# Normalized tokens of four chunks of six, turned by VectorE squares and memory in place of TensorE

## The chip, the cores and the metric

One Trainium2 chip, one of its cores. The metric is device time in microseconds (us) for one execution of the whole kernel; lower is better.

## The reference

The input is x of shape (8, 128, 48, 48): 8 batches, 128 channels, N = 2304 positions. Everything is float32. What is computed, cut to what matters:

```python
# layer 0: causal attention over positions, with a group norm ahead of it
x0 = concat([gn(x), position embeddings])             # 160 channels
q, k, v = (leaky_relu(W @ x0 + b) for W, b in ...)    # 128 channels each
x = x + softmax(causal(q.T @ k / sqrt(128))) @ v
# layer 1: full attention of the normalized tokens with themselves, no weights
t = x as (8, 2304, 128)
n = layernorm(t)                                      # over the 128 channels of a token
t = t + softmax(n @ n.T) @ n
# then a recurrent feed-forward layer with batch norm
t = t + scan(sigmoid(wx_t + y @ V.T)), wx = batchnorm(layernorm(t) @ W.T)
```

The change concerns `n`. Full attention needs it in two arrangements: with tokens on partitions (for the product of the probabilities with n) and with channels on partitions (for the scores n @ n.T).

## The kernel before, in words

A core's memory has 128 partitions. A batch's 2304 positions are cut into NQ = 6 chunks of QC = 384 columns, a chunk into QB = 3 blocks of P = 128. For each batch the kernel runs causal attention (class `Causal`) and then full attention (class `Full`); after all batches a recurrence (from line 1499) runs in 96 segments.

**Order of work.** The order is written out by the program itself (`manual_schedule`, line 788). `stream` (lines 1466 to 1476) lists all items, and each item is one 128 x 384 block of scores: `begin` issues the score product on TensorE and the exponential on ScalarE, and LAG = 3 items later `product` issues the product with the values. Causal chunk j has 3(j+1) items, so the chunks grow from 3 to 18 items. All other work is put in chains of steps: `st.add` takes a list of (function, cost on TensorE, [(engine, us), ...]); class `Stream` (line 548) keeps an estimated clock, `st.now`, and estimated free times of the engines, and `st.tick`, called after each item, issues up to two steps whose time has come. `st.finish(chain)` issues all that is left of a chain at once, `st.advance(chain, n)` as many steps as are needed for n to be done. A step's estimate only decides where its instructions stand in the queues of the engines; what an instruction really waits for is its semaphores. Each engine, and SyncE (SP), which issues most DMAs, works through its queue in order.

**Causal attention.** `Causal.begin` (1022): scores of keys on partitions by queries in columns (L1032), exp on ScalarE into a tile p (L1034, six buffers), for the blocks on the diagonal a multiplication by triu on GpSimd (L1037). `Causal.product` (1041): the output o gathers v times p (L1043), and VectorE adds p to a running sum acc (L1054, L1058). The projections of the following chunks (`project`, 869) run beside it as chains. When a chunk is done, `after` (1061) makes a chain that takes the chunk to normalized tokens. For chunks 0 to 4 (`far`) the output is turned to tokens on partitions by VectorE, which turns each 32 x 32 square in its place (`turn_result`, L972), and by a store and four loads that move the squares (`token_major`, L980 and L986: o_d_c and to_c). Then:

- `turn` (1081) and `sums` (1087): the softmax denominators, with a small product on TensorE (dn, L1091);
- `residual` (1099): y, the tile t1t that was loaded with x at L1079, gets the attention's output divided by its denominator (L1105), and its mean and variance per token (L934 to L937);
- `rooted` (1111): the inverse root on GpSimd (L943);
- `normed` (1114): the normalized tokens, c["y"], into the tokens-on-partitions copy x_hat[b][0], tile xhT (L948);
- `back` (1122): the same with channels on partitions, into x_hat[b][1], tile xh: three 128 x 128 transposes on TensorE into the tile tb in PSUM (L953), and a copy on ScalarE (L1124);
- `shifted` (1126): GpSimd adds 1 to xhT and takes 1 from t1t (L1128, L1129).

**Full attention.** `Full.begin` (1244) issues the scores from xh alone, as weights and as columns (L1269), and `Full.product` the product with xhT (L1291). As the scores are symmetric, blocks under the diagonal are not computed again: VectorE turns squares (L1236), stores (e, L1187) and loads (g, L1179) bring the mirrored blocks, which L1279 uses; those inside a chunk go through GpSimd's queue (m, gm, L1217, L1221). While j is 0, `begin` calls `st.finish(normed_chunks[b, chunk])` ahead of each block (1247), so all steps of a causal chunk's chain are issued by the time that full attention first uses that chunk. Its own chains (`after`, 1299) make the token's second layer norm and the product with W.

`chunk_tile` (692) hands out working tiles and sees that the chain of the tile's former holder has been issued far enough.

Of the kernel before, what the change touches and what calls it, by code (L numbers as in the profile page):

```python
# [14 lines left out]
F32 = mybir.dt.float32  # L15
# [589 lines left out]
def fast_path(ctx: ExitStack, tc: tile.TileContext, x, pe, w_ffn, out, x_tok, w_qkv, w_pos, v_t, gamma_beta, flag):  # L605
    nc = tc.nc
    B, C, H, W = x.shape
    N = H * W
    P = 128
# [3 lines left out]
    QC = 384  # L613
    NQ = N // QC
    QB = QC // P
# [6 lines left out]
    dpool = ctx.enter_context(tc.tile_pool(name="dram", bufs=1, space=DRAM))  # L622
# [17 lines left out]
    SQ = 32  # L640
    R = P // SQ
# [25 lines left out]
    with ExitStack() as actx:  # L667
# [19 lines left out]
        def psum_t(name):  # L687
            return ps_t.tile([P, CH], F32, tag="t", name=name)
# [3 lines left out]
        def chunk_tile(tag, name, holder=None, steps=0, bufs=2):  # L692

            if holder is not None:
                before = holders.setdefault(tag, deque([({}, 0)] * bufs))
                old, n = before.popleft()
                before.append((holder, steps))
                if "chain" in old:
                    st.advance(old["chain"], n)
            return (work if bufs == 2 else work1).tile([P, QC], F32, tag=tag, name=name)  # L700
# [228 lines left out]
        def moments(y, name, tag):  # L929

            mv = small.tile([P, QB, 2], F32, tag=f"mv_{tag}", name=f"mv_{name}")
            for g in range(QB):
                s6 = small.tile([P, 6], F32, tag=f"st_{tag}", name=f"st_{name}_{g}")
                nc.vector.bn_stats(s6, y[:, ts(g, P)])  # L934
                nc.vector.bn_aggr(mv[:, g, :], s6)
            ve = small.tile([P, QB], F32, tag=f"ve_{tag}", name=f"ve_{name}")
            nc.vector.tensor_scalar_add(ve, mv[:, :, 1], 1e-5)  # L937
            return mv, ve
# [11 lines left out]
        def transposed(src, name):  # L950
            tp = psum_t(name)
            for g in range(QB):
                nc.tensor.transpose(tp[:, ts(g, P)], src[:, ts(g, P)], ident)  # L953
            return tp
# [9 lines left out]
        def turn_result(o, name, holder, blocks_first):  # L964

            ot = chunk_tile("o", f"ot_{name}", holder, 1)
            dst, src = ot.rearrange("p (a g c) -> p a g c", a=R, g=QB), o[:, :QC]
            if blocks_first:
                dst, src = dst.rearrange("p a g c -> p g a c"), src.rearrange("p (g a r) -> p g a r", a=R, g=QB)
            else:  # L970
                src = src.rearrange("p (a g r) -> p a g r", a=R, g=QB)
            nc.vector.transpose(dst, src)  # L972
            return ot

        def token_major(holder, ot, name, tag, steps):

            d = dpool.tile([P, QC], F32, tag=f"o_{tag}", name=f"o_d_{name}")

            def store():
                nc.sync.dma_start(d, ot)  # L980

            def load():
                holder["o"] = to = chunk_tile(tag, f"to_{name}", holder, steps, bufs=1)
                src = d.rearrange("(k r) (a f) -> a r k f", r=SQ, a=R)
                for r in range(R):
                    nc.sync.dma_start(to[ts(r, SQ)].rearrange("r (k f) -> r k f", k=R), src[r])  # L986

            return [(store, 0.0, [("", 5.0)]), (load, 0.0, [("", 5.0)])]

        def block_of(to, g):  # L990

            return to.rearrange("p (k g c) -> p g k c", g=QB, c=SQ)[:, g]

        def by_block(tile_ap):

            return tile_ap.rearrange("p (g a r) -> p a g r", a=R, g=QB)
# [4 lines left out]
        t1_tok, x_hat, normed_chunks = {}, {}, {}  # L1001

        class Causal:
# [57 lines left out]
            def after(self, j, o):  # L1061
                b = self.b
                cols = ts(j, QC)
                acc = self.sums.pop(j)[1]
                c = self.whose.pop(j)

                far = CAUSAL_FAR and j < NQ - 1
                if far:
                    ot = turn_result(o, f"c_{b}_{j}", c, False)
                    at = st.then(st.now, [("DVE", 0.57)])  # L1070
                    through = token_major(c, ot, f"c_{b}_{j}", "toc", 5)
                else:
                    o_sb = chunk_tile("o", f"oc_{b}_{j}", c, 3)
                    nc.scalar.copy(by_block(o_sb), o[:, :QC].rearrange("p (a g r) -> p a g r", a=R, g=QB))
                    at = st.then(st.now, [("ACT", 0.5)])
                    through = []

                y = t1p.tile([P, QC], F32, tag="t1t", name=f"t1t_{b}_{j}")
                nc.sync.dma_start(y, x_tok[b, j])  # L1079

                def turn():
                    ta = chunk_tile("ta", f"ta_{b}_{j}", bufs=1)
                    nc.vector.transpose(ta, acc)
                    c["parts"] = small.tile([P, R * QB], F32, tag="parts", name=f"parts_{b}_{j}")
                    nc.vector.tensor_reduce(c["parts"], ta.rearrange("p (k c) -> p k c", c=SQ), AX.X, ALU.add)

                def sums():

                    tp = psum_t(f"dn_{b}_{j}")
                    k = R * QB  # L1090
                    nc.tensor.matmul(tp[:, :k], same.rearrange("p a c -> p (a c)"), c["parts"], start=True, stop=True)  # L1091
                    own = small.tile([P, R, QB], F32, tag="ownc", name=f"ownc_{b}_{j}")
                    nc.vector.tensor_mul(own.rearrange("p a g -> p (a g)"), tp[:, :k], mine.rearrange("p a g -> p (a g)"))
                    ri = small.tile([P, QB], F32, tag="ric", name=f"ric_{b}_{j}")
                    nc.vector.tensor_reduce(ri, own.rearrange("p a g -> p g a"), AX.X, ALU.add)
                    nc.vector.reciprocal(ri, ri)
                    c["ri"] = ri

                def residual():
                    to = None if far else transposed(o_sb, f"oc_t_{b}_{j}")  # L1100
                    for g in range(QB):
                        yg = y[:, ts(g, P)]
                        if far:
                            yg = yg.rearrange("p (k c) -> p k c", k=R)
                        nc.vector.scalar_tensor_tensor(  # L1105
                            yg, block_of(c["o"], g) if far else to[:, ts(g, P)], c["ri"][:, g : g + 1], yg, ALU.mult, ALU.add
                        )
                    t1_tok[b, j] = y
                    c["mv"], c["ve"] = moments(y, f"c{b}_{j}", "l1")

                def rooted():
                    c["rs"] = root(c["ve"], f"c{b}_{j}", "l1")

                def normed():
                    if j == 0:
                        x_hat[b] = (
                            big.tile([P, NB, P], F32, tag="xhT", name=f"xhT_{b}"), big.tile([P, N], F32, tag="xh", name=f"xh_{b}")
                        )
                    c["y"] = x_hat[b][0][:, QB * j : QB * (j + 1), :].rearrange("p g c -> p (g c)")
                    normalize(c["y"], t1_tok[b, j], c["mv"], c["rs"])  # L1120

                def back():
                    tp = transposed(c["y"], f"tb_{b}_{j}")
                    nc.scalar.copy(x_hat[b][1][:, cols], tp[:, :QC])  # L1124

                def shifted():

                    nc.gpsimd.tensor_scalar_add(c["y"], c["y"], 1.0)  # L1128
                    nc.gpsimd.tensor_scalar_add(t1_tok[b, j], t1_tok[b, j], -1.0)  # L1129

                c["chain"] = normed_chunks[b, j] = st.add([
                    *through[:1],
                    (turn, 0.0, [("DVE", 1.05)]),
                    *through[1:],
                    (sums, 0.15, [("DVE", 0.55)]),
                    (residual, 0.0 if far else 0.35, [("DVE", 2.6)]),
                    (rooted, 0.0, [("POOL", 0.9)]),
                    (normed, 0.0, [("DVE", 1.1)]),
                    (back, 0.35, [("ACT", 0.5)]),
                    (shifted, 0.0, [("POOL", 1.2)]),  # L1140
                ], max(at, st.free["DVE"]) + 0.2 - st.now)

        class Full:
# [334 lines left out]
        for n in range(len(stream) + LAG):  # L1478
            if n < len(stream):
                part, j, what, first, last = stream[n]  # L1480
# [5 lines left out]
            if n >= LAG:  # L1486
                part, j, what, first, last = stream[n - LAG]
# [16 lines left out]
    with ExitStack() as rctx:  # L1504
# [32 lines left out]
        a = rc.tile([P, 1], F32, tag="bn_a", name="bn_a")  # L1537
        rsqrt(rc, a, mv[:, 1:2], 1e-5, "bn")
        nc.vector.tensor_mul(a, a, gb[:, 0:1])
        c = rc.tile([P, 1], F32, tag="bn_c", name="bn_c")  # L1540
# [17 lines left out]
        prev, warm, y = [], [], [None] * G  # L1558
# [129 lines left out]
```

## Time and profile before

| | |
|---|---|
| Time, median of 3 runs | 1742.51 us (1737.38 to 1744.68) |
| Profiled execution: time | 1747.17 us |
| Profiled execution: span from first to last instruction | 1745.5 us |
| Granted TensorE clock | 0.995 |
| Instructions | 22,358 |
| DMA packets | 214,697, of which 93,889 under 512 B |
| HBM read, written | 157.31 MB, 119.61 MB |
| TensorE transposes tb (L953) | 144, in 48 groups of three |
| ScalarE copies of tb (L1124) | 48 of 479 ns each |

The profile names the engines PE (TensorE), PEld (its weight loads), DVE (VectorE), ACT (ScalarE), POOL (GpSimd) and SP (SyncE). A row of a group of instructions has line, engine, operation, "written tile <- read tiles", shape and count, then busy us and mean ns of one, then the idle time of the engine just before them and what ended it. PE lists one product of float32 as two matmul records; a transpose of 128 x 128 is one. A letter q behind an engine's name stands for its instruction queue, so SPq is where SyncE issues DMAs. A wait for several semaphores is put down to the one that came last.

### The profile page before, as it was taken

How to read it: one execution, taken by the hardware profiler on the slowest of the kernel's cores; microseconds unless marked ns; L12 is line 12 of the kernel's file. 1: busy time of each engine (PE TensorE's matmuls, PEld its weight loads, DVE VectorE, ACT ScalarE, POOL GpSimd, SP SyncE). 2: the span in 40 equal slices, each digit the busy share in tenths (PEclk: the TensorE clock that was granted, in tenths of full speed). 3: DMA queues.
4: the chain of work that ended last, by engine and by line, in shares of the span. 5: the costliest groups of instructions: out<-in, count | busy, mean ns of one | idle time of the engine just before them, and what ended most of it. 6: DMA issues, size and time to landing. Idle time of an engine off the chain costs nothing.

```text
span 1745.5 us, 22358 instructions
## 1 busy us (share of the span) xinstructions
PE 1705.2 (98%) x6338; PEld 1094.7 (63%) x6339; DVE 1190.0 (68%) x3259; ACT 699.5 (40%) x1332; POOL 453.9 (26%) x637
## 2 busy tenths in 40 slices
PE   9999999999999999999999999999999999999986
PEld 6666666666666666666666666666666666666565
DVE  5865578656876478755786568864787656864457
ACT  3344334443344423443344433444244432444345
POOL 1232123311233112321224112332123212241206
PEclk9999999999999999999999999999999999999998
DMA  3317763378424874178632784338831686127858
GB/s 120 114 31 213 227 191 100 106 204 235 145 71 138 226 232 112 49 204 230 199 100 81 200 242 144 100 111 230 242 114 55 183 239 198 52 84 205 229 208 219
DMA packets 214697, 278.54 MB, mean 160 GB/s; under 512 B 93889, under 2 KB 178786, under 8 KB 214052
## 3 DMA queue, kind: packets, MB, share of 16 engines
q1 hardware_dynamic: 204396, 255.11, 50.0%
q0 software_dynamic: 9936, 21.51, 4.4%
q8 instruction: 52, 0.85, 0.2%
q14 instruction: 81, 0.66, 0.1%
q10 hardware_dynamic: 232, 0.40, 0.1%
HBM read 157.31 MB, written 119.61 MB: 159 GB/s over the span
## 4 chain that ended last, share of the span: by engine, by line
PE 89%; DMA 5%; DVE 2%; POOL 1%; SPq 1%; issue 1%; ACT 0%; POOLq 0%; DVEq 0%; ACTq 0%
PE s L1032 17%; PE o L1043 17%; PE s L1269 16%; PE o L1291 16%; PE o L1279 10%; DMA g<-e 3%; PE pj L895 3%; PE z L1601 2%; PE o L1287 2%; PE wx L1369 2%; DMA t2x<-t_d 1%; PE pj L898 1%; POOL gm L1221 1%; PE tb L953 1%; PE of_t L953 1%; SPq L1187 1%
## 5 line engine op out<-in xcount | busy, mean ns | idle before, releaser
L1271 ACT ACTIVATE p<-s,shift 128x384 f32<-128x384 f32 (+2 forms) x504 | 274.8, 551 | 544.5 <-PE s L1269 480.1
L1034 ACT ACTIVATE p<-s 128x384 f32<-128x384 f32 (+2 forms) x504 | 230.2, 460 | 395.3 <-PE s L1032 331.2
L1043 PE MATMUL o<-p,vT 128*128 128x384 f32 (+2 forms) x1008 | 377.8, 456 | 4.6 <-POOL p L1037 4.6
L1032 PE MATMUL s<-q,k 128*128 128x384 f32 (+2 forms) x1008 | 381.4, 460 | 0.1
L1269 PE MATMUL s<-xh 128*128 128x384 f32 (+2 forms) x1008 | 378.3, 457 | 0.0
L1291 PE MATMUL o<-p,xhT 128*128 128x384 f32 (+2 forms) x1008 | 367.6, 456 | 0.0
L1279 PE MATMUL o<-g,xhT 128*128 128x384 f32 x720 | 277.7, 489 | 9.7 <-DMA g<-e 9.7
L1236 DVE STREAM_TRANSPOSE t<-p 128x384 f32<-128x384 f32 x360 | 183.9, 550 | 146.3 <-DMA e<-t 75.0
L1291 PEld LDWEIGHTS o<-p,xhT 128*128 128x128 f32 x1008 | 189.2, 190 | 118.8 <-ACT p L1271 0.3
L1043 PEld LDWEIGHTS o<-p,vT 128*128 128x128 f32 x1008 | 186.7, 190 | 115.8 <-POOL p L1037 8.9
L1269 PEld LDWEIGHTS s<-xh 128*128 128x128 f32 x1008 | 184.9, 190 | 105.9
L1032 PEld LDWEIGHTS s<-q,k 128*128 128x128 f32 x1008 | 179.3, 190 | 86.5 <-issue 2.2
L1058 DVE TENSOR_TENSOR acc<-acc,p 128x384 f32<-128x384 f32 (+2 forms) x408 | 209.7, 514 | 26.7 <-DVE acc L1058 1.6
L1279 PEld LDWEIGHTS o<-g,xhT 128*128 128x128 f32 x720 | 131.6, 191 | 89.8 <-DMA g<-e 14.5
L1037 POOL TENSOR_TENSOR p<-p,triu 128x128 f32<-128x128 f32 x144 | 72.2, 505 | 288.7 <-ACT p L1034 287.9
L1221 POOL DMA_DIRECT2D gm<-m x192 | 107.4, 564 | 71.5 <-PE s L1269 25.1
L1128 POOL TENSOR_SCALAR xhT<-xhT 128x384 f32<-128x384 f32 x48 | 57.4, 1195 | 242.4 <-PE tb L953 242.4
L1343 POOL TENSOR_TENSOR roots<-ve_f,mhalf 128x3 f32<-128x3 f32 x48 | 42.3, 880 | 254.8 <-DVE ve_f L937 254.6
L1217 POOL DMA_DIRECT2D m<-tm x48 | 28.9, 602 | 205.4 <-DVE tm L1204 205.0
L1370 DVE TENSOR_TENSOR scale<-wx,scale 128x384 f32<-128x384 f32 x46 | 25.6, 557 | 78.9 <-PE wx L1369 62.9
L895 PE MATMUL pj<-xn,wT 128*128 128x384 f32 x192 | 77.9, 488 | 1.5 <-DVE xn L888 1.5
L902 DVE TENSOR_TENSOR q<-pj,pb 128x384 f32<-128x384 f32 x48 | 26.7, 556 | 69.4 <-PE pj L895 69.4
(248 smaller groups left out, 1732.9 us busy)
## 6 DMA issues: line engine op xcount, KB each, us to landing
e<-t SPq DMA_DIRECT2D x480, 144.0 KB
g<-e SPq DMA_DIRECT2D x120, 576.0 KB
pb<-posb_d SPq DMA_DIRECT2D x42, 576.0 KB
t1t<-in_x_tok_dram SPq DMA_DIRECT2D x48, 192.0 KB
m<-tm POOLq DMA_DIRECT2D x48, 192.0 KB, 4.7
gm<-m POOLq DMA_DIRECT2D x192, 48.0 KB, 3.4
t_d<-tt SPq DMA_DIRECT2D x184, 48.0 KB
t2x<-t_d SPq DMA_DIRECT2D x46, 192.0 KB
```

The source lines that it names most:

```text
L895: nc.tensor.matmul(ps[:, :QC], wT[:, j, :], xn, start=True, stop=True)
L1032: nc.tensor.matmul(s[:, off:QC], keys[b][:, ts(m, P)], queries[b, j][:, off:], start=True, stop=True)
L1034: nc.scalar.activation(p[:, off:], s[:, off:QC], AF.Exp, scale=SCALE)
L1037: nc.gpsimd.tensor_mul(p[:, off : off + P], p[:, off : off + P], triu)
L1043: nc.tensor.matmul(o[:, off:QC], vals[b][:, ts(m, P)], p[:, off:], start=first, stop=last)
L1058: nc.vector.tensor_add(a[:, off:], a[:, off:], p[:, off:])
L1221: nc.gpsimd.dma_start(gm[ts(r, SQ)].rearrange("c a q r -> c a (q r)"), d.rearrange("(a c) b f -> b c a f", a=R)[r])
L1236: nc.vector.transpose(t[:, :, :, g, :].rearrange("p b j r -> p j b r"), p.rearrange("p (j b r) -> p j b r", j=QB, b=R))
L1269: nc.tensor.matmul(s[:, off:QC], xh[:, ts(m, P)], xh[:, j * QC + off : (j + 1) * QC], start=True, stop=True)
L1271: nc.scalar.activation(p[:, off:], s[:, off:QC], AF.Exp, bias=shift)
L1279: nc.tensor.matmul(out_ap, xhT[:, QB * i + g, :], p, start=first, stop=last)
L1291: nc.tensor.matmul(o[:, off:QC], xhT[:, what[1], :], p[:, off:], start=first, stop=last)
```

## The change

In `Causal.after`, chunks 0 to 3 (`j < NQ - 2`) no longer use `back`. In its place come four steps, `ways`: `turn_normed` turns the 32 x 32 squares of the normalized tokens on VectorE into a new tile yt (one buffer); `shifted` follows, as before; `put` stores yt to memory in four DMAs of 32 partitions each, in runs of 32 elements (128 B); `get` loads it back in three DMAs, one for each block of 128 columns and all 128 partitions, again in runs of 32 elements, straight into xh. Chunks 4 and 5 keep `back` and `shifted`. Memory x_d has two places, for even and odd chunks.

```diff
+                def turn_normed():
+                    c["yt"] = chunk_tile("yt", f"yt_{b}_{j}", c, len(through) + 6, bufs=1)
+                    nc.vector.transpose(
+                        c["yt"], c["y"]
+                    )
+
+                def put():
+                    c["x_d"] = dpool.tile([R, QB * R, SQ, SQ], F32, tag=f"x_d_{j % 2}", name=f"x_d_{b}_{j}")
+                    for k in range(R):
+                        nc.sync.dma_start(
+                            c["x_d"][k].rearrange("f c r -> c f r"), c["yt"][ts(k, SQ)].rearrange("c (f r) -> c f r", r=SQ)
+                        )
+
+                def get():
+                    src = c["x_d"].rearrange("k (g a) c r -> g (a c) k r", g=QB)
+                    for g in range(QB):
+                        dst = x_hat[b][1][:, ds(j * QC + g * P, P)]
+                        nc.sync.dma_start(dst.rearrange("p (k r) -> p k r", k=R), src[g])
+
+                ways = [
+                    (turn_normed, 0.0, [("DVE", 0.57)]),
+                    (shifted, 0.0, [("POOL", 1.2)]),
+                    (put, 0.0, [("", 4.0)]),
+                    (get, 0.0, [("", 4.0)]),
+                ]
...
                     (normed, 0.0, [("DVE", 1.1)]),
-                    (back, 0.35, [("ACT", 0.5)]),
-                    (shifted, 0.0, [("POOL", 1.2)]),
+                    *(ways if j < NQ - 2 else [(back, 0.35, [("ACT", 0.5)]), (shifted, 0.0, [("POOL", 1.2)])]),
                 ], max(at, st.free["DVE"]) + 0.2 - st.now)
```

R is 4 and SQ is 32 (lines 640 and 641), so R x SQ = P.

More of the change, by code (lines that the diff above doesn't have):

```diff
@@ L1120, in normed, with shifted @@
                     normalize(c["y"], t1_tok[b, j], c["mv"], c["rs"])
+                def shifted():
+                    nc.gpsimd.tensor_scalar_add(c["y"], c["y"], 1.0)
+                    nc.gpsimd.tensor_scalar_add(t1_tok[b, j], t1_tok[b, j], -1.0)
                 def back():
@@ L1124, in back @@
                     nc.scalar.copy(x_hat[b][1][:, cols], tp[:, :QC])
-                def shifted():
-                    nc.gpsimd.tensor_scalar_add(c["y"], c["y"], 1.0)
-                    nc.gpsimd.tensor_scalar_add(t1_tok[b, j], t1_tok[b, j], -1.0)
+                def turn_normed():
[20 more added lines that the diff above has]
+                ]
                 c["chain"] = normed_chunks[b, j] = st.add([
```

## The prediction

> **What bounds the kernel now.** I read the page's totals first, then the chain that ended last, then the groups of instructions with shapes kept apart, and last the timeline, the waits and the stretches around one changed step.
>
> The totals and the shares of the chain:
>
> ```profile
> PE 1705.2 (98%) x6338; PEld 1094.7 (63%) x6339; DVE 1190.0 (68%) x3259; ACT 699.5 (40%) x1332; POOL 453.9 (26%) x637
> PE 89%; DMA 5%; DVE 2%; POOL 1%; SPq 1%; issue 1%; ACT 0%; POOLq 0%; DVEq 0%; ACTq 0%
> ```
>
> TensorE is busy for 98% and owns 89% of the chain. "Busy" overcounts, as ends of pipelined matmuls are modelled, so I looked at gaps instead. Between causal chunk starts of consecutive batches about 204 us pass, and in 460:535 (causal attention of the third batch and the start of its full attention) TensorE has no gap in any stretch. The columns are length, then busy time and instructions of PE, PEld, DVE, ACT and POOL, the clock, the DMA share and GB/s:
>
> ```profile
> 460.00:475.00 15.00, 15.00 (x54) 9.33 (x53) 14.23 (x44) 6.48 (x13) 3.73 (x7) 1.00 0.20 63
> 475.00:490.00 15.00, 15.00 (x59) 9.77 (x58) 13.00 (x36) 5.74 (x13) 4.13 (x6) 1.00 0.41 135
> 490.00:505.00 15.00, 15.00 (x53) 9.24 (x52) 12.95 (x37) 8.21 (x15) 4.87 (x4) 1.00 0.39 113
> 505.00:520.00 15.00, 15.00 (x58) 9.50 (x57) 12.20 (x35) 6.24 (x14) 5.76 (x7) 1.00 0.14 41
> 520.00:535.00 15.00, 15.00 (x59) 9.68 (x58) 9.51 (x34) 7.48 (x15) 6.12 (x6) 1.00 0.04 14
> ```
>
> Two things to see: whatever leaves TensorE's queue here shortens the stretch by its slot, as no wait stands around it; and VectorE, at 14.23 of 15, is the next engine, while the DMA engines are mostly idle just where the change uses them.
>
> The groups of the step that goes, and the nearest rows to what comes:
>
> ```profile
> L953 PE MATMUL tb<-ident,xhT 128*128 128x128 f32 x144 | 23.9, 274 | 0.2 <-DVE xhT L948 0.2
> L1124 ACT COPY xh<-tb 128x384 f32<-128x384 f32 x48 | 23.0, 479 | 19.3 <-PE tb L953 19.3
> L1083 DVE STREAM_TRANSPOSE ta<-acc 128x384 f32<-128x384 f32 x48 | 27.1, 564 | 0.0
> ```
>
> The step on TensorE's timeline, for the fourth chunk of that batch:
>
> ```profile
> 518.64 0.81 PE L1043 MATMUL o<-p,vT 128*128 128x384 f32 x2
> 519.29 0.49 PE L953 MATMUL tb<-ident,xhT 128*128 128x128 f32 x3
> 519.61 0.81 PE L1032 MATMUL s<-q,k 128*128 128x384 f32 x2
> ```
>
> The three transposes hold the queue from 519.29 to 519.61, 0.32 us, not the 3 x 274 ns of their durations: the next score product starts before they end.
>
> **What the Trainium skill says.** "TensorE: Matmul & The Clock Gate", section Part 4 (PE-mode transpose), gives about 275 ns for a 128x128 transpose within a kernel and says that the result lands in PSUM and must be copied. The trace agrees (274 ns, and L1124's copy), but that is latency; the slot above decides, 0.107 us each. "VectorE: DVE Perf Modes", section The three transpose paths, says VectorE turns only 32x32 blocks and stays in SBUF. The trace has this operation (564 ns); the rest of the turn must therefore be done by the stores and loads. "DMA: Bandwidth & Descriptors", section Specifications, calls 512 B the least transfer for line rate. The added runs are 128 B; the trace of before already moves 25,128 packets of 128 B (mostly the t2c stores) at a mean of 13 ns each, so they are inefficient but short. The same page, section Two DMAs through the same engine are not ordered, says that a load of what a store wrote must wait for the store's completion before it is issued: here SyncE's queue waits, as it does at L986 for the store of L980.
>
> **The change, part by part.** It meets 4 chunks x 8 batches = 32 instances.
>
> *Removed on TensorE.* 96 transposes in 32 slots. 31 of them have 0.32 to 0.33 us from the first transpose to the next product; the first batch's first chunk has 0.68 us with 0.24 us idle ahead of it, as the queue ran dry there. Sum 10.8 us from first transpose to next product; I count 10.5, since the dry spot will keep part of its wait. All lies on the path.
>
> *Removed on ScalarE.* 32 copies x 0.479 = 15.3 us. Nothing: ScalarE is 40% busy, and its products lie ready 3.2 us (median) ahead of the matmul that takes them. PSUM slots of the transposes become freer, also worth nothing.
>
> *Added on VectorE.* 32 x 0.564 = 18.0 us, 2.26 us a batch against some 1.3 us less TensorE time. From 460 to 520 VectorE is busy for 52.4 of 60 us; with 2.0 more in 58.7 it would be at 93%. It lags, then catches up: its gaps in this stretch are 0.85 us at 484, 0.62 at 497, 0.70 at 507 and this one,
>
> ```profile
> 522.52 0.17 DVE L1093 TENSOR_TENSOR ownc<-dn,mine 128x12 f32<-128x12 f32 x1 [3.52 <-PE dn L1091]
> ```
>
> about one behind each of the four new transposes, which I place where the transposes on TensorE now stand (near 481, 500, 509 and 519). So the lag rises by at most 0.6 us at a time. What is queued behind it is the sums over p (L1058); they free p's buffers for ScalarE. They start up to 2.75 us after their product already, and ScalarE waits for that without TensorE feeling it:
>
> ```profile
> ACT p L1034 <- DVE acc L1054: 36.2, 19, 2.0
> ```
>
> A lag of 0.6 us more against a lead of some 3 us: nothing. If this cover were gone, all 18.0 us would land on the path. Both ends are kept: 0 and +18.0.
>
> *Moved on GpSimd.* The two additions (1.2 and 1.27 us) now wait for the VectorE transpose in place of the TensorE one, at the same point of the plan. GpSimd sat idle 242 us before L1128; behind it queue triu's products (L1037), which in chunks 2 to 6 end 1.1 us or more, mostly about 2 us, ahead of their matmul. Nothing, or a few tenths a batch.
>
> *Added on SyncE and DMA.* 7 DMAs a chunk, 224 in all. Nearest issues: four loads of L986 in 1.74 us. So 4 x 0.44 for the stores and 3 x 0.44 to 0.9 for the loads: 3.1 to 4.4 us of SyncE a chunk, in stretches where it issues every few us only:
>
> ```profile
> 499.90 1.75 SPq L986 DMA_DIRECT2D to_c<-o_d_c  x4
> 501.70 0.43 SPq L1397 DMA_DIRECT2D t2s_d<-t2c  x1
> 502.17 1.32 SPq L1079 DMA_DIRECT2D t1t<-in_x_tok_dram  x1
> 505.34 0.32 SPq L980 DMA_DIRECT2D o_d_c<-ot_c  x1
> 510.56 1.74 SPq L986 DMA_DIRECT2D to_c<-o_d_c  x4
> 512.35 0.43 SPq L1079 DMA_DIRECT2D t1t<-in_x_tok_dram  x1
> ```
>
> Packets: 4 stores x 384 + 3 loads x 512 = 3072 of 128 B a chunk; at 13 ns over 16 engines 2.5 us of DMA time, 10 us a batch, where the share is 0.04 to 0.41. Reads of 128 B are not in the trace; I bound them by 13 and 26 ns (the latter the mean of 384 B packets), which changes nothing at this load. The stores wait for VectorE and the loads for the stores, in SyncE's order; behind them stand the next chunks' o_d_c, to_c and t1t. to_c of the fifth chunk is issued at 510.56 and used at 523.47, so a hold of a few us on SyncE is covered.
>
> *The new latency.* x_hat's columns must be in place when full attention uses the chunk. Only the fourth is near: transposed at 519.3, the plan puts the stores 2.4 us later (521.7) and the loads 4.15 us after that (525.8); with up to 4 us to land, 530. Full attention starts its products at 523.7 and reaches the chunk's first block, the tenth, at 534.93. Five us are left: nothing. The fifth and sixth chunk keep the old way.
>
> *Sum.* 10.5 us less. The profiled execution has a span of 1745.5 us and a time of 1747.17; 1736.7 is left. It lies 4.7 us above the median of the runs, 1742.51, so there I expect **1732.0 us**, 0.6% less. About 0.5% (8.7 us) is what a measurement of this kernel can tell from no change, so the gain is near that line.
>
> **Rivals.**
> 1. *VectorE becomes the bound in the causal stage.* For it: 14.23 of 15 us busy, and no gap from 460 to 484. Against: the four gaps above, and that TensorE shows no gap. If half of the 18.0 us comes through, 1732.0 + 9.0 = 1741: no change.
> 2. *The end of each full attention is paced by memory, and swallows what was won.* For it: TensorE's waits there are for loads of mirrored tiles, with the DMA share about 0.7.
>
> ```profile
> PE o L1279 <- DMA g<-e: 9.7, 12, 3.4
> ```
>
> Against: 9.7 us in all, and these transfers begin with the stage itself, so they move up with it. If it held, 1742.
> 3. *The fourth chunk's loads come late* (the slower side). Place: the tenth block of full attention. Stores and loads need each other's completion on one queue, and the pieces are 128 B. From 5 us of extra delay on, each us late costs TensorE 1 us a batch. At 8 us late: 3 x 8 = 24 us, less 10.5: 1756. Against: a DMA share of 0.04 there.
>
> That the change doesn't do what it says I exclude: 96 transposes leave the queue by the code.
>
> **Chances.** The forecast 0.62, with 1727 to 1736 as its own spread (the plan's clock shifts, so that small waits fall differently); rival 1 0.15; rival 2 0.10; rival 3 0.13. Of the forecast's part some 0.10 lies above 1733.8, within 0.5%. So faster 0.52, within 0.35 (0.10 + 0.25), slower 0.13. The range goes from 1726 to 1746: it holds the forecast and rivals 1 and 2, and leaves out rival 3 and a little of the low side.
>
> **What would show it.** Right: 48 transposes of tb left in place of 144, TensorE instructions fewer by 96, still no gap from the causal stage on, batches shorter by about 1.3 us; the VectorE transposes followed by shrunken gaps. Wrong: waits of L1032 or L1043 on ScalarE behind acc (rival 1); longer waits at L1279 (rival 2); waits of L1269 on a DMA into xh (rival 3), or to_c loads so held up on SyncE that L1105 waits for them.

## The result and the profile after

Over 12 runs each, the median went from 1744.45 us to 1739.3 us; the ratio is 0.9976 with a 95% interval of 0.9954 to 0.9997. By this ratio, which compares the means, that is 4.2 us less (0.5 to 8.0), where 10.5 us were forecast; the medians are 5.2 us apart. The kernel became faster, but a gain of 10.5 us lies outside the interval.

The one profiled pair flatters the change: 1747.17 us before, 1735.51 us after, 11.7 us apart. The profile of before holds two stretches of 3.4 us at half TensorE clock near its end, the one after none there (both also end with 13 to 15 us at half clock). Over all runs below, a mean granted clock lower by 0.001 goes with 1.0 to 2.0 us more time, about 1.5 us in the larger sets, and the runs of one kernel lie between 0.989 and 0.997, `e7_five` apart. So times are compared here as ratios over many runs, and beside them at one clock.

The totals of the page after, and the shares of its chain:

```profile
PE 1692.1 (98%) x6243; PEld 1083.3 (62%) x6243; DVE 1205.0 (70%) x3291; ACT 684.4 (39%) x1300; POOL 445.2 (26%) x637
PE 89%; DMA 5%; DVE 2%; SPq 1%; POOL 1%; issue 1%; ACT 1%; DVEq 0%; POOLq 0%; ACTq 0%
```

TensorE is still the bound; 96 transposes are gone (95 records), VectorE is busy for 15 us more. The groups of the step, after (L1129 is the copy that was L1124, L1133 the new VectorE transpose):

```profile
L953 PE MATMUL tb<-ident,xhT 128*128 128x128 f32 x48 | 7.9, 272 | 0.0
L1129 ACT COPY xh<-tb 128x384 f32<-128x384 f32 x16 | 7.7, 479 | 6.2 <-PE tb L953 6.2
L1133 DVE STREAM_TRANSPOSE yt<-xhT 128x384 f32<-128x384 f32 x32 | 18.2, 570 | 0.0
```

The same 75 us of the third batch, in 15 us stretches (columns as in the prediction):

```profile
457.00:472.00 15.00, 15.00 (x54) 9.44 (x53) 14.20 (x44) 6.57 (x14) 3.59 (x6) 1.00 0.19 58
472.00:487.00 15.00, 15.00 (x57) 9.62 (x56) 13.39 (x35) 5.49 (x12) 3.88 (x5) 1.00 0.55 170
487.00:502.00 15.00, 15.00 (x51) 9.12 (x51) 12.64 (x39) 7.84 (x14) 1.11 (x1) 1.00 0.43 105
502.00:517.00 15.00, 15.00 (x54) 9.33 (x53) 13.54 (x37) 5.57 (x12) 8.33 (x9) 1.00 0.48 93
517.00:532.00 15.00, 15.00 (x59) 9.68 (x58) 9.74 (x33) 7.43 (x14) 4.43 (x5) 1.00 0.34 73
```

TensorE again has no gap here. From the first causal score product of a batch to its first full one, the stage takes 85.14 us in the second to eighth batch, where it took 86.68: the slots were won. What was lost must lie behind that point, and TensorE's waits in full attention, by total, times and longest, show it:

```profile
PE o L1304 <- DMA g<-e: 6.1, 6, 2.4
PE s L1294 <- ACT xh L1129: 4.5, 8, 0.6
```

The second line was not there before. It is one wait per batch, for a copy into xh, and L1129 is the old way, which only the fifth and sixth chunk still take. The timeline of TensorE, third batch, after:

```profile
538.08 0.49 PE L953 MATMUL tb<-ident,xhT 128*128 128x128 f32 x3
539.14 0.91 PE L1294 MATMUL s<-xh 128*128 128x384 f32 x2 [0.57 <-ACT xh L1129]
```

and the same two instructions before (the view ends at 542.00, so that it holds one of the product's two records):

```profile
541.38 0.49 PE L953 MATMUL tb<-ident,xhT 128*128 128x128 f32 x3
541.71 0.49 PE L1269 MATMUL s<-xh 128*128 128x384 f32 x1
```

These are the transposes of the sixth chunk. Before, 0.33 us later comes a score product of the block ahead of that chunk's first, which needs nothing of them. After, 14 score products of full attention have become 15: the next product is of the sixth chunk's first block, which needs these very columns. It waits until the transposes have drained and ScalarE has copied them: 1.06 us from the first transpose to the product in place of 0.33, so 0.73 us lost, in 8 batches 5.9 us. 10.8 less 5.9 is 4.9 us.

The transposes could not simply have stood one block earlier, at 536.79. What they turn was ready only at 537.86, as VectorE had waited for the inverse root on GpSimd, here and in six other batches:

```profile
537.00 0.86 DVE L948 TENSOR_SCALAR xhT<-t1t,mv_c,rs_c 128x128 f32<-128x128 f32 x3 [0.58 <-POOL rs_c L943]
```

The root's input was ready at 534.10, but it started at 536.07, behind the issue of four loads on GpSimd (lines below, at `e4_ahead`). Before, it started 0.15 us after its input, ahead of the same loads:

```profile
536.27 0.88 POOL L943 TENSOR_TENSOR rs_c<-ve_c,mhalf 128x3 f32<-128x3 f32 x1 [2.62 <-DVE ve_c L937]
```

### The profile page after: what moved, and what is told of

It reads as the page before. It is cut to its first block, busy times and chain, and to the rows that moved or that the text cites. A ratio compares the mean times of both kernels' runs of the same rounds, so it can differ in the third digit from the quotient of the medians.

```text
span 1733.7 us, 22462 instructions
## 1 busy us (share of the span) xinstructions
PE 1692.1 (98%) x6243; PEld 1083.3 (62%) x6243; DVE 1205.0 (70%) x3291; ACT 684.4 (39%) x1300; POOL 445.2 (26%) x637
## 4 chain that ended last, share of the span: by engine, by line
PE 89%; DMA 5%; DVE 2%; SPq 1%; POOL 1%; issue 1%; ACT 1%; DVEq 0%; POOLq 0%; ACTq 0%
PE s L1032 17%; PE o L1043 17%; PE s L1294 15%; PE o L1316 15%; PE o L1304 11%; PE pj L895 3%; DMA g<-e 2%; DMA t2x<-t_d 2%; PE z L1626 2%; PE o L1312 2%; PE pj L898 2%; PE wx L1394 2%; SPq L1212 1%; POOL gm L1246 1%; PE of_t L953 1%
## 5 line engine op out<-in xcount | busy, mean ns | idle before, releaser
L1058 DVE TENSOR_TENSOR acc<-acc,p 128x384 f32<-128x384 f32 (+2 forms) x408 | 209.2, 513 | 22.5 <-ACT p L1034 1.2
L1037 POOL TENSOR_TENSOR p<-p,triu 128x128 f32<-128x128 f32 x144 | 67.2, 471 | 437.1 <-ACT p L1034 436.9
L1124 POOL TENSOR_SCALAR xhT<-xhT 128x384 f32<-128x384 f32 x48 | 62.2, 1296 | 106.7 <-DVE yt L1133 56.8
```

Source lines behind the costliest of these rows:

```text
L1037: nc.gpsimd.tensor_mul(p[:, off : off + P], p[:, off : off + P], triu)
L1058: nc.vector.tensor_add(a[:, off:], a[:, off:], p[:, off:])
```

## The experiments

My theory: the slots were won in full, and the added work costs nothing, but with the transposes of the other chunks gone TensorE arrives at the sixth chunk before the plan has placed that chunk's own transposes, so that `st.finish` places them directly ahead of their first use. The rivals: the added VectorE or memory work gives the gain back, in proportion to its amount; or nothing is lost, and the granted clock blurs the comparison.

The table has all runs: the ratio to the kernel before with its interval, and the difference at a clock of 0.995 by a straight line through the runs of each kernel (the kernel before, beside them on each of three chips: 1743.9 us for `e0_before` to `e4_ahead`, 1742.7 for `e5_late` to `e8_removed_ahead`, 1742.0 for the last two). By the scatter about the lines such a difference is known to about 1.5 us either way, that of `e8_removed_ahead`, from six runs, to 4 us or more.

| run | ratio | 95% interval | at one clock |
|---|---|---|---|
| e0_before | 0.9987 | 0.9974 to 1.0 | -0.1 us |
| e2_removed | 0.9935 | 0.9911 to 0.9959 | -8.3 us |
| e3_two | 0.9989 | 0.9974 to 1.0005 | -2.2 us |
| e4_ahead | 0.9934 | 0.9908 to 0.9959 | -12.2 us |
| e5_late | 1.0041 | 1.0025 to 1.0056 | +7.4 us |
| e6_added | 0.9996 | 0.9984 to 1.0008 | -0.9 us |
| e7_five | 1.0189 | 1.0162 to 1.0216 | none near 0.995 |
| e8_removed_ahead | 0.9934 | 0.9908 to 0.996 | -11.7 us |
| e9_changed | 0.9978 | 0.9964 to 0.9991 | -3.1 us |
| e10_ahead | 0.9947 | 0.9932 to 0.9963 | -9.4 us |

**The kernel before, against itself.** No edit.

> The kernel before itself, as a control of what a comparison can tell. Every theory: ratio 1.000 within about 0.2%. If the granted clock is what blurs the comparison, its executions differ by up to 10 us and the longer ones have the lower granted clock; this gives the clock of the kernel before beside the 0.990 to 0.996 of the changed kernel.

Measured 0.9987: a comparison of one kernel with itself can be off by about 2 us. Its 22 runs go from 1737.62 to 1749.62 us, at clocks from 0.997 to 0.992.

**The transposes taken away, nothing put in.**

```diff
-                    (turn_normed, 0.0, [("DVE", 0.57)]),
                     (shifted, 0.0, [("POOL", 1.2)]),
-                    (put, 0.0, [("", 4.0)]),
-                    (get, 0.0, [("", 4.0)]),
+                    (filled, 0.0, [("POOL", 0.6)]),
...
+                def filled():
+                    nc.gpsimd.memset(x_hat[b][1][:, cols], 0.125)
```

> The transposes of four chunks and their copies are taken away and nothing of the squares, stores and loads put in: GpSimd fills these columns with a constant, so the scores of full attention are not the reference's. My theory (the slots were won in full, 10.8 us; but TensorE now reaches the sixth chunk before its chain does, so that its transposes stand directly ahead of the block that needs them, 0.73 us a batch from the second batch on, 5.1 us): the wait of 0.57 us for the copy into xh stays in 7 batches, the time is about 5.7 us under the kernel before (0.9967). Rival (the added VectorE work or the stores and loads give the gain back): no such wait, 10.8 us under (0.9938).

Measured 0.9935. Each theory has half of it: the ratio is the rival's (0.9938, where mine gave 0.9967), but the wait is there in 7 batches, as mine said, in a kernel that has no VectorE transpose and no added store or load:

```profile
PE s L1295 <- ACT xh L1129: 4.0, 7, 0.6
```

So the added work does not make this wait; taking the transposes away does. But the time is lower than my sum, at one clock by 2.6 us, over six runs only, and I have no cause for it.

**Two chunks of six.**

```diff
-                    *(ways if j < NQ - 2 else [(back, 0.35, [("ACT", 0.5)]), (shifted, 0.0, [("POOL", 1.2)])]),
+                    *(ways if j < 2 else [(back, 0.35, [("ACT", 0.5)]), (shifted, 0.0, [("POOL", 1.2)])]),
```

> The new way for two chunks of six. My theory: the loss is a step that comes whole with the first chunk, so 16 slots win 5.5 us and 7 batches lose 0.73 us each, 5.1 us: no change (1.000). Rival (a loss that grows with the added work): half of the changed kernel's gain, 2 to 3 us under (0.9988). If nothing was lost and the comparison only blurs it: 5.5 us under (0.9969).

Measured 0.9989, at one clock 2.2 us less. The profile has the wait 7 times, 4.0 us in all, with half of the added work: a step, not a slope. The time does not show it: the interval holds my 1.000 and the rival's 0.9988, and the measured value is the rival's.

**A chain's rest issued one block ahead.**

```diff
-                    st.finish(normed_chunks[b, what[1] // QB])
+                    st.finish(normed_chunks[b, min(what[1] + 1, NB - 1) // QB])
```

> The changed kernel with the rest of a chunk's chain issued one block ahead of its first use in place of directly ahead of it. My theory: the transposes of the sixth chunk again stand one block ahead, the wait of 0.57 us is gone in all batches, and the time is about 10.5 us under the kernel before (0.994), some 6 us under the changed kernel. Rival (VectorE is late with the normalized tokens of the sixth chunk): TensorE waits for them ahead of the transposes, 0.6 us or more a batch, and the time stays where the changed kernel's was, about 0.9976.

Measured 0.9934, and measured again beside the changed kernel on one chip below. The wait for the copy is gone. TensorE's timeline of the third batch in this kernel:

```profile
536.39 0.49 PE L953 MATMUL tb<-ident,xhT 128*128 128x128 f32 x3
536.72 0.81 PE L1294 MATMUL s<-xh 128*128 128x384 f32 x2
```

VectorE, which the rival expected to be late, is not: the edit also brings the sixth chunk's inverse root forward. In the changed kernel it stood behind the issue of four loads on GpSimd:

```profile
533.83 2.23 POOL L1246 DMA_DIRECT2D gm<-m  x4
536.07 0.89 POOL L943 TENSOR_TENSOR rs_c<-ve_c,mhalf 128x3 f32<-128x3 f32 x1
```

and here it stands ahead of them:

```profile
533.86 0.88 POOL L943 TENSOR_TENSOR rs_c<-ve_c,mhalf 128x3 f32<-128x3 f32 x1 [1.32 <-DVE ve_c L937]
```

**The kernel before with the sixth chunk's transposes one block later.** All work is kept; in the order that the planner writes, only the transposes and the copy of the sixth chunk move, in each batch by one block.

```diff
-                    (normed, 0.0, [("DVE", 1.1)]),
+                    (normed, 0.0, [("DVE", 1.1), ("", 1.3 if j == NQ - 1 else 0.0)]),
```

> The kernel before, all its work kept, with one step moved: the transposes and the copy of the sixth chunk stand directly ahead of the block that needs them in place of one block ahead (1.3 us more in the plan of that chunk alone). My theory (this place alone costs 0.73 us a batch): a wait of 0.57 us for the copy into xh in all 8 batches, and 5.9 us over the kernel before (1.0034). Rival (the wait appears in the changed kernel but costs nothing, since the end of full attention waits for memory anyway): the wait is there and the time is that of the kernel before.

Measured 1.0041 (4.4 to 9.8 us more), with the wait in every batch:

```profile
PE s L1269 <- ACT xh L1124: 4.5, 8, 0.6
```

This place alone costs what my theory says, 5.9 us, within the interval, and the end of full attention does not hide it.

**The added work alone**, beside the old transposes.

```diff
                     (turn_normed, 0.0, [("DVE", 0.57)]),
+                    (back, 0.35, [("ACT", 0.5)]),
...
-                        dst = x_hat[b][1][:, ds(j * QC + g * P, P)]
+                        dst = c["yt"][:, ts(g, P)]
...
-                    c["yt"] = chunk_tile("yt", f"yt_{b}_{j}", c, len(through) + 6, bufs=1)
+                    c["yt"] = chunk_tile("yt", f"yt_{b}_{j}", c, len(through) + 9, bufs=1)
```

> The added work alone: the VectorE transpose, the four stores and the three loads of four chunks, beside the old transposes and copies, which alone write xh; the loads go into yt and nothing uses them. My theory: VectorE and memory are covered; the time is that of the kernel before, or up to 2.5 us over it (1.000 to 1.0014), by the difference between the kernel with the transposes taken away and the changed kernel at the same clock less the 0.73 us of one batch. In the first batch the sixth chunk is late by the plan, 0.7 us of this. Rival (VectorE's 18 us come through at least half): 9 us over or more (1.005).

Measured 0.9996. In the first batch alone the sixth chunk's transposes stand directly ahead of their use, as the expectation has it. As the loads end in yt, VectorE even waits for them ahead of the next chunk's transpose, and still TensorE's waits show nothing of it:

```profile
L1133 DVE STREAM_TRANSPOSE yt<-xhT 128x384 f32<-128x384 f32 x32 | 18.3, 571 | 30.8 <-DMA yt<-x_d 30.8
```

**Five chunks**, with the edit of e4_ahead.

```diff
-                    *(ways if j < NQ - 2 else [(back, 0.35, [("ACT", 0.5)]), (shifted, 0.0, [("POOL", 1.2)])]),
+                    *(ways if j < NQ - 1 else [(back, 0.35, [("ACT", 0.5)]), (shifted, 0.0, [("POOL", 1.2)])]),
```

> The new way for five chunks, the fifth too, with the chain's rest issued one block ahead as in the run ahead. By my theory and the rival of a late load alike the point from which latency decides is in this chunk: its tokens are normalized about 9 us into full attention, and its first block is used about 15 us into it. Transpose, stores and loads need 0.6 us, then twice 2 to 4 us to land, and what SyncE has queued: 5 to 10 us, so TensorE waits 0 to 4 us a batch for xh. The slots of the fifth chunk win 2.6 us. From 13 us under the kernel before (0.9925) to 20 us over it (1.0115); a wait of L1269's line on a DMA into xh shows which.

Measured 1.0189, 33 us more. The mechanism of the prediction's third rival is real; it decides one chunk later than that rival had it:

```profile
PE s L1294 <- DMA xh<-x_d: 28.4, 8, 4.1
```

3.6 us a batch on average. The waits are 28.4 us; the slots win 13.4 us. The rest follows the waits: in the records, TensorE's clock falls to one half around the end of seven of the eight, four times for 6.8 and three times for 3.4 us. Only the wait of the seventh batch, 3.02 us, has none at its end; another 3.4 us come 19 us after it, behind a wait of 2.2 us for something else (gn_mv). That is 41 us at half clock, and costs half of it, 20.5 us. 28.4 + 20.5 - 13.4 is 35.5 us. On TensorE's timeline, third batch, the records after the wait are almost twice as long:

```profile
544.13 0.81 PE L1316 MATMUL o<-p,xhT 128*128 128x384 f32 x2
548.59 1.65 PE L1294 MATMUL s<-xh 128*128 128x384 f32 x2 [3.65 <-DMA xh<-x_d]
550.02 1.49 PE L1316 MATMUL o<-p,xhT 128*128 128x384 f32 x2
```

The mean clock of these runs is 0.981 to 0.987.

**The transposes taken away, and the rest one block ahead.** The edits of e2_removed and e4_ahead.

> The transposes and copies of four chunks taken away, nothing put in (GpSimd fills the columns with a constant, so the scores are not the reference's), and the rest of a chain issued one block ahead. My theory: without the wait for the copy; 11 to 13 us under the kernel before (0.993), within 2.5 us of the changed kernel issued one block ahead, as the added work is covered. Rival (the added work costs): 5 us or more under that kernel (0.990).

Measured 0.9934, at one clock 11.7 us less. The two runs of the kernel with the added work and the same edit, e4_ahead and e10_ahead, are at -12.2 and -9.4, on other chips. So no cost of the stores, the loads and VectorE's 18 us is seen, but six runs cannot exclude one of 4 us; e6_added is the sharper bound (2.8 us less to 1.4 us more than the kernel before).

**The changed kernel, and it with the rest one block ahead, on one chip.** No further edit.

> The changed kernel again, beside the next run on the same chip, since their two ratios so far came from different chips and their intervals touch. My theory: 10.8 us of slots and about 0.25 us a batch of other work, less 5.9 us for the place of the sixth chunk's transposes: 0.996 to 0.998. If the first comparison was blurred by the granted clock and nothing is lost: 0.994.

> The changed kernel with a chain's rest issued one block ahead, again. My theory: 0.993 to 0.994, 5 to 7 us under the changed kernel of the same call. Rival (the first run was lucky in its granted clock): within 2 us of the changed kernel.

Measured 0.9978 and 0.9947; medians 1738.1 and 1733.42 us, 4.7 us apart, at one clock 6.3 us. The intervals do not overlap (0.9963 against 0.9964). The version with the edit beats both kernels.

## Why the prediction was wrong

*What bounds the kernel* held: no gap on TensorE in the causal stage, before or after.

*The slots* held. The causal stage is shorter by 1.54 us a batch, where four slots are 1.31. Of the rest, 0.14 us is a denominators' product (L1091) that now falls behind the stage's border and so is no gain; 0.09 us I did not trace. In the first batch it is 2.3 us: slots of 1.66 us, 0.24 us of the dry spot ahead of one of them, and a rest that I did not trace.

*VectorE* held. The gap of 3.52 us that was shown is now

```profile
522.46 0.17 DVE L1093 TENSOR_TENSOR ownc<-dn,mine 128x12 f32<-128x12 f32 x1 [2.88 <-PE dn L1091]
```

smaller by 0.64 us. One reading of the prediction was wrong here, that about one gap stands behind each new transpose. Two of them, at 507.86 and 517.79, have no gap of VectorE between them, so its lag could reach two transposes, 1.1 us, and not 0.6 at most. ScalarE's wait for the sums of L1054 did not rise with it (it was 36.2 us; that for the sums of L1058 went from 7.0 to 9.2):

```profile
ACT p L1034 <- DVE acc L1054: 24.1, 13, 1.9
```

*SyncE and DMA* held: 98,304 packets of 128 B more, at 13.0 ns each on average, reads too (the bound was 13 to 26). The seven issues of a chunk fit between the old ones, for the fourth chunk:

```profile
510.67 1.91 SPq L986 DMA_DIRECT2D to_c<-o_d_c  x4
512.74 1.48 SPq L1148 DMA_DIRECT2D xh<-x_d  x3
514.26 0.50 SPq L1079 DMA_DIRECT2D t1t<-in_x_tok_dram  x1
518.39 1.87 SPq L1140 DMA_DIRECT2D x_d<-yt  x4
521.77 1.48 SPq L1148 DMA_DIRECT2D xh<-x_d  x3
```

Its loads are issued at 521.77 and its first block is used at 529.60, 7.8 us later, where 9.1 us had been forecast; TensorE does not wait for them.

*The step that failed* is the end of "The new latency": "The fifth and sixth chunk keep the old way." They keep their instructions, not their place, on TensorE and on GpSimd. The sum priced what leaves TensorE's queue and took the rest of the order as fixed, with "the plan's clock shifts, so that small waits fall differently" as a spread of a few us to both sides, and it looked on GpSimd at the moved additions alone. But a removed step with a planned 0.35 us on TensorE lets the plan's clock reach full attention sooner, while the sixth chunk's chain does not shorten with it. That chain's transposes stood only one block ahead of their first use; they lost that one block in every batch (e2_removed has the loss without any added work in 7, e5_late has it without any other change). On GpSimd the chain's root fell behind the four loads, and so from the second batch on the tokens came too late for the old place. The lines that would have shown it were in the trace of before: the transposes at 541.38 and, one block on, the product that reads them. The price, 5.9 us, is missing from the sum.

*The rivals.* Neither of the first two took the gain. e6_added excludes VectorE's 9 us. Against the second stands e10_ahead, which at one clock is 9.4 us below the kernel before with the same end of full attention, and e5_late, whose loss that end does not hide; the waits for mirrored tiles themselves tell nothing, as two profiles of one kernel differ by as much (before 9.7 and, in e0_before, 7.2 us; changed 6.1 and, in e9_changed, 10.1). That the times these two rivals gave, 1741 and 1742 us, lie nearer to the measured 1739.3 than the forecast is a coincidence. The third does not act in the changed kernel, but acts in e7_five.

**What stays open.** I did not run a kernel with the planned 0.35 us kept. But the planner stands in the kernel, and its order can be worked out without the chip. The kernel before with the planned 0.35 us of the four chunks set to zero, and nothing else changed, has the sixth chunk's transposes directly ahead of their use in seven batches, the same as e2_removed: the lost 0.35 us is enough. The changed kernel with 0.35 us planned for `turn_normed` has them there in seven batches too: its new steps alone shift the plan as well. Neither was run.

e2_removed was faster than the sum by 2.6 us, with the wait in its profile. At one clock it is 5.2 us below the changed kernel of e9_changed, where one wait less is worth 0.7. The two ran on different chips, and the same kernel, as e4_ahead and as e10_ahead, differs by 2.8 us between these chips; a small cost of the added work is not excluded by this pair. And the profiles of full attention differ from batch to batch by up to 7 us (116.4 to 123.6 us outside the first and the last batch and e7_five), so that 0.73 us a batch can be read there only as a wait, not from the stage's length.

## What to carry to other kernels

When a step leaves the engine that is the bound, ask of each step that stays how far ahead of its first use it stands, and whether that distance was made by the time now removed: a transpose with a copy that stood one block ahead cost its slot of 0.33 us, and directly ahead of its use 1.06 us. Where an order is written by a planner, a changed cost moves steps that the diff does not name, on every engine; compare the order of the instructions before summing durations. Here, issuing the rest of a chain one block ahead of its use, and not at it, won 4.7 us (6.3 at one clock).

## What the runs showed of the hardware

In e7_five, waits of TensorE of 3.2 to 4.1 us were paid more than once: around the end of each came 3.4 or 6.8 us at half clock, in which a pair of 384-column records takes 1.49 us in place of 0.81. The wait of 3.02 us in the same profile was followed by none, and so were the waits of 0.57 us of the changed kernel. "TensorE: Matmul & The Clock Gate" of the Trainium skill, section Why this matters for your kernels, advises against idle gaps over about 3 us for this reason. The trace agrees in the main, but length alone does not decide it: in e8_removed_ahead and e10_ahead, 3.4 us at half clock stand at the end of waits of 2.3 to 2.4 us.
